# The third layer's block-diagonal products as quarters of the array, its messages and the projection by halves of the rows

## The chip, the cores and the metric

One Trainium2 chip; the program runs on one of its cores. The metric is the device time of one execution in microseconds (us). Of the kernel before there are three timed runs and one profiled execution.

## The reference

Four graph layers follow each other on x, which is 8 graphs x 2048 nodes x 64 features, with one shared 0/1 adjacency of 2048 x 2048. Each layer normalises, rectifies, computes and adds to x. The change is in the third layer and in what the third layer's last step prepares for the fourth. Cut to these:

```python
def _L2_gnn_ref(causal_vars, adj_matrix, intervention_value, W1, b1, W2, b2, intervention_idx):
    v = causal_vars.at[:, intervention_idx].set(intervention_value)
    for _ in range(3):
        effects = jnp.einsum('nm,bmd->bnd', adj_matrix, v)
        h = jnp.concatenate([v, effects], axis=-1)
        h = jax.nn.relu(jnp.einsum('bnk,dk->bnd', h, W1) + b1)
        v = jnp.einsum('bnk,dk->bnd', h, W2) + b2
    return v

def _L3_gnn_ref(x, adj, weight, a, bias):
    h = jnp.einsum('bni,io->bno', x, weight)
    e_src, e_dst = h @ a[:D, 0], h @ a[D:, 0]      # D = 64
    e = jax.nn.leaky_relu(e_src[:, :, None] + e_dst[:, None, :], negative_slope=0.2)
    ...                                            # times adj, softmax, times h

h = jnp.maximum(_layernorm(x, axis=-1), 0.0)
x = x + _L2_gnn_ref(h, adj, ...)
h = jnp.maximum(_layernorm(x, axis=-1), 0.0)
x = x + _L3_gnn_ref(h, adj, ...)
```

## The kernel before

**Layout.** Two graphs of 64 features make a pair, which fills the 128 partitions. There are NP = 4 pairs, called q. Features by node are kept as v(q), 128 partitions x 2048 nodes; the transposed form, by node, is u(t), 128 nodes x 512 columns (four pairs of 128), for each of NT = 16 tiles of nodes. A weight of 64 x 64 is placed twice on the diagonal of a 128 x 128 matrix (w1v, w1e, w2), with zeros elsewhere, so that one product serves both graphs of a pair.

**A step of the third layer.** The step's messages are v times the weight for neighbours. For each tile t, `messages` makes four products into one bank pn (128 nodes x 512) and empties it by one copy (step 0, taking turns between ScalarE and VectorE, L141 and L143) or by one addition on VectorE with the constant row later (steps 1 and 2, L1416). `split` then makes two parts of u, u_n_hi on ScalarE (L201) and u_n_lo on VectorE (L202), whose products with the adjacency run in one pass each. `adj_product` goes over NC = 4 chunks of 512 nodes. For a chunk it holds four banks pp0 to pp3, one for each pair. `first` begins them with the node's own product (w1v, or later in steps 1 and 2, which folds w2 and w1v); then come 16 tiles x 2 parts x 4 pairs of products with the adjacency (u_n in the text). `done` empties the four banks by Relu on ScalarE (L1444) into v, and at once makes the messages of the next step for the chunk's four tiles. In the third step `done` applies w2 instead, into banks named p2 (p in the trace), which VectorE adds to x (L1456), stores x and calls `Scores.chunk`.

**The projection.** `Scores.chunk` normalises the chunk for the fourth layer (center, to_rows, from_rows, the banks named bank) and multiplies each tile with wide, which holds weight3 twice on the diagonal and four columns for the scores: 132 columns, two pairs in one bank pw. Copies bring the features to rows(t) and the scores to scores; both go to f_rows in memory, from where the fourth layer gathers. `Scores.end` sums hn over all nodes and multiplies the sum with wide.

**The order.** A scheduler orders the instructions of each engine before the run, from the program's order and the buffers; the order on the chip is then fixed. Beside steps 0 and 1 runs a generator `neighbours`, one piece at every second tile of adjacency: it gathers 128 rows of the adjacency (L1486, POOL's queue, 1 MB each) into one of two buffers, and finds each row's neighbours by passes over 2048 columns on VectorE: L1490, L1494, then L1500 (eight highest) and L1503 (strike them out) in turns, and L1507 (copy). Fifteen tiles of rows pass through it.

**Buffers.** The banks pn and p2 have two buffers each. pw takes pn's, bank takes p2's.

All products on TensorE go through one helper, so they stand at L135 whatever they do; they are told apart by the names of their tiles. The listing shows the functions that the change touches.

Of the kernel before, what the change touches and what calls it, by code (L numbers as in the profile page):

```python
# [7 lines left out]
F = mybir.dt.float32  # L8
# [5 lines left out]
OP = mybir.AluOpType  # L14
# [5 lines left out]
P = 128  # L20
NB = 8
N = 2048
D = 64
NP = NB // 2
NT = N // P
R = P // NP
CW = 512
# [54 lines left out]
def columns(tile, s):  # L82

    return tile.rearrange("n (q s f) -> n q s f", q=NP, s=2)[:, :, s]
# [11 lines left out]
class Kernel:  # L96
# [36 lines left out]

    def mm(self, out, lhsT, rhs, start=True, stop=True):
        self.nc.tensor.matmul(out, lhsT, rhs, start=start, stop=stop)  # L135

    def copy(self, out, in_):

# [1232 lines left out]
    def layer2(self, slots):  # L1371
        nc, tc, a = self.nc, self.tc, self.a
        v = Halves(slots, "v", ("q0", "q1"), False)
        u = Halves(slots, "u", ("q2", "q3"), True)

        with (
            tc.tile_pool(reuse_waits="tile", name="k2", bufs=1) as k,
            tc.tile_pool(reuse_waits="tile", name="steps", bufs=2) as w,
            tc.tile_pool(reuse_waits="tile", name="steps_ps", bufs=1, space=PSUM) as ps,
            tc.tile_pool(reuse_waits="tile", name="steps_ps2", bufs=2, space=PSUM) as ps2,  # L1380
        ):
            w1v = self.block_diag(k, a["W1T"][:D], "w1v")
            w1e = self.block_diag(k, a["W1T"][D:], "w1e")
            w2 = self.block_diag(k, a["W2T"], "w2")

            w2n = k.tile([P, P], F, name="w2n")
            pw = ps2.tile([P, NP, P], F, name="pn")
            nc.tensor.transpose(pw[:, 0], w2, self.ident)
            nc.vector.tensor_copy(w2n, pw[:, 0])
            pw = ps2.tile([P, NP, P], F, name="pn")  # L1390
            self.mm(pw[:, 0], w2n, w1v)
            self.mm(pw[:, 1], w2n, w1e)
            self.mm(pw[:, 2], self.col("b2").to_broadcast([P, P]), w1e)
            self.mm(pw[:, 3, :1], w1v, self.col("b2"))
            later = k.tile([P, 3, P], F, name="later")
            nc.vector.tensor_copy(later, pw[:, :3])
            b1 = k.tile([P, 1], F, name="b1")
            nc.vector.tensor_add(b1, pw[:, 3, :1], self.col("b1"))
            own = [w1v, later[:, 0], later[:, 0]]
            seen = [w1e, later[:, 1], later[:, 1]]  # L1400
            bias = [self.col("b1"), b1, b1]
            full = [P, NP, P]
            for q in range(NP):
                nc.vector.tensor_copy(v(q)[:, 0:1], self.col("iv"))

            def messages(step, tiles):

                for t in tiles:
                    pn = ps2.tile(full, F, name="pn")
                    for q in range(NP):  # L1410
                        self.mm(pn[:, q], v(q)[:, t * P : (t + 1) * P], seen[step])
                    to = u(t).rearrange("n (q f) -> n q f", q=NP)
                    if step == 0:
                        self.copy(to, pn)
                    else:
                        nc.vector.tensor_add(to, pn, later[:, 2].unsqueeze(1).to_broadcast(full))  # L1416

            near = self.neighbours(k, slots) if self.short else iter(())
            last = Scores(self, slots, k, w, ps2) if self.short else None
            turn = [0]  # L1420

            def after(ch, m, at):
                turn[0] += 1
                if turn[0] % 2:
                    next(near, None)

            messages(0, range(NT))
            for step in range(3):
                if step == 2:
                    for _ in near:  # L1430
                        pass
                u_n = Split(slots, "u_n")
                for t in range(NT):
                    self.split(u_n, t, u(t))

                def first(ch, out, step=step):
                    s = slice(ch * CW, (ch + 1) * CW)
                    for q in range(NP):
                        self.mm(out[q], own[step], v(q)[:, s], stop=False)

                def done(ch, out, step=step):
                    s = slice(ch * CW, (ch + 1) * CW)
                    for q in range(NP):
                        nc.scalar.activation(v(q)[:, s], out[q], AF.Relu, bias=bias[step])  # L1444
                    if step < 2:
                        messages(step + 1, range(ch * TC, (ch + 1) * TC))
                        return
                    if last is not None:
                        x = last.x
                        nc.sync.dma_start(x, self.xs[2][ch])  # L1450
                    else:
                        x = self.load_x(w, 2, ch, bufs=1)
                    for q in range(NP):
                        p2 = ps2.tile([P, CW], F, name="p2")
                        self.mm(p2, w2, v(q)[:, s])
                        nc.vector.scalar_tensor_tensor(  # L1456
                            x[:, q], p2, self.col("b2"), x[:, q], op0=OP.add, op1=OP.add
                        )
                    self.store_x(2, ch, x)
                    if last is not None:  # L1460
                        last.chunk(ch)

                self.adj_product(u_n, w, ps, done, first=first, after=after)
            if last is not None:
                last.end()
# [371 lines left out]
class Scores:  # L1837
# [3 lines left out]
    def __init__(self, kern, slots, k, w, ps):  # L1841
        self.kern, self.nc, self.w, self.ps = kern, kern.nc, w, ps
        nc, a = self.nc, kern.a
        self.x, self.xr, self.sq, self.hn, self.total, self.rows = kern.last_slots(slots)

        self.wide = k.tile([P, P + 4], F, name="wide")
        nc.gpsimd.memset(self.wide, 0.0)
        self.sums = k.tile([P, NP, NC], F, name="sums")
        for s in range(2):
            half = slice(s * D, (s + 1) * D)  # L1850
            nc.sync.dma_start(self.wide[half, half], a["weight3"])
        wt = k.tile([D, 2, D], F, name="wt")
        for s in range(2):
            nc.sync.dma_start(wt[:, s], a["weight3T"])
        aa = k.tile([D, 2], F, name="aa")
        nc.sync.dma_start(aa, a["a2"])
        pa = self.bank()
        kern.mm(pa[:, :2], wt.rearrange("o s i -> o (s i)"), aa)
        for s in range(2):
            half = slice(s * D, (s + 1) * D)  # L1860
            for i in range(2):
                c = P + 2 * i + s
                nc.vector.tensor_copy(self.wide[half, c : c + 1], pa[half, 1 - i : 2 - i])

    def bank(self):
# [2 lines left out]
    def chunk(self, ch):  # L1868
        nc, kern = self.nc, self.kern
# [8 lines left out]
        kern.norm(ch, self.x, self.xr, self.sq, std, self.bank, write)  # L1878
        for t in range(ch * TC, (ch + 1) * TC):
            i = t - ch * TC  # L1880
            scores = kern.scores[:, t].rearrange("n (i q s) -> n q i s", i=2, s=2)
            for g in range(2):
                pn = self.ps.tile([P, 2, 256], F, name="pw", tag="pn")
                for j in range(2):
                    kern.mm(
                        pn[:, j, : P + 4], self.hn[:, 2 * g + j, i * P : (i + 1) * P], self.wide
                    )
                to = self.rows(t)[:, 2 * g * P : 2 * (g + 1) * P]
                kern.copy(to.rearrange("n (j c) -> n j c", j=2), pn[:, :, :P])
                nc.vector.tensor_copy(  # L1890
                    scores[:, 2 * g : 2 * g + 2],
                    pn[:, :, P : P + 4].rearrange("n q (i s) -> n q i s", i=2),
                )
            to = kern.f_rows[t * P : (t + 1) * P]
            nc.sync.dma_start(to[:, : NB * D], self.rows(t))
            nc.sync.dma_start(to[:, NB * D :], kern.scores[:, t])

    def end(self):
        nc = self.nc
        sums = self.w.tile([P, NP], F, name="all_sums", bufs=1)  # L1900
        nc.vector.tensor_reduce(sums, self.sums, axis=AX.X, op=OP.add)
        pt = self.bank()
        for q in range(NP):
            self.kern.mm(
                pt[:, q * P : (q + 1) * P], sums[:, q : q + 1].to_broadcast([P, P]),
                self.wide[:, :P],
            )
        nc.vector.tensor_copy(self.total, pt)


class Near:
# [345 lines left out]
```

## Time and profile before

| what | value |
|---|---|
| three timed runs | 2223.14, 2223.89, 2229.41 us; median 2223.89 |
| profiled execution | 2223.47 us, span 2221.7 us, clock 0.905 |
| TensorE, products | 1967.9 us busy, 7530 |
| TensorE, weight loads | 1187.1 us busy |
| VectorE, ScalarE, POOL | 1115.2, 708.9, 727.9 us busy |
| own products (w1v, later) | 96 passes of 512 columns |
| p (w2) | 32 passes of 512 columns |
| messages pn (w1e, later) | 384 passes of 128 columns |
| projection pw | 128 passes of 132 columns |

The span runs from the first to the last instruction of the profiled execution; 1.8 us lie around it. Busy time is a mean over four layers with different limits, so a cost is read from its stage: the third layer lies between about 1385 and 1925 us. A pass is one TensorE instruction; an fp32 product takes two. The mean duration of a pass in a group is from its start to its result and overlaps the next one's; the rate is read from the starts. In the timeline a row is a run of equal instructions: its start, the time it was busy, and how many; in brackets the idle time before it and what ended it.

### The profile page before, as it was taken

The numbers are of one execution on the slowest core, as the hardware profiler recorded it, in microseconds if no ns is written. First come the engines' busy times: TensorE is split into PE (matmuls) and PEld (weight loads), VectorE is DVE, ScalarE is ACT, GpSimd is POOL, SyncE is SP. The second block draws the span as 40 slices with busy tenths as digits, with TensorE's granted clock in tenths as the row PEclk, the third lists the DMA queues.
The fourth block names the chain that finished last, engine by engine and source line by source line (L and its number), as shares of the span: only waits on it lengthen the run. The fifth ranks groups of instructions, "written<-read, shape, count | busy, mean of one in ns | idle before, by whom it ended". The sixth has DMA issues, their size and how long they took to land.

```text
span 2221.7 us, 21410 instructions
## 1 busy us (share of the span) xinstructions
PE 1967.9 (89%) x7530; PEld 1187.1 (53%) x7530; DVE 1115.2 (50%) x1980; ACT 708.9 (32%) x1347; POOL 727.9 (33%) x609
## 2 busy tenths in 40 slices
PE   5877899987879989999999998998999999679873
PEld 1454766652226766353353532876777666345432
DVE  7846767744762032524425244988302222349762
ACT  6401455543444342020110200433434333258300
POOL 0012066755320002726537175011000000277760
PEclk8856899996777989999999998999999999789996
DMA  8231133451122453040130402456333443375655
GB/s 318 71 101 27 52 94 112 126 159 67 38 76 86 131 130 118 0 139 13 54 99 0 114 1 82 149 191 218 103 123 123 144 151 124 131 199 164 180 158 201
DMA packets 107742, 253.76 MB, mean 114 GB/s; under 512 B 19600, under 2 KB 19744, under 8 KB 100320
## 3 DMA queue, kind: packets, MB, share of 16 engines
q1 hardware_dynamic: 90000, 185.22, 26.1%
q0 software_dynamic: 17616, 67.00, 10.1%
q8 instruction: 63, 1.03, 0.2%
q14 instruction: 63, 0.52, 0.1%
HBM read 218.37 MB, written 33.81 MB: 114 GB/s over the span
## 4 chain that ended last, share of the span: by engine, by line
PE 57%; DVE 8%; POOL 7%; DMA 6%; issue 5%; ACT 3%; SPq 1%; POOLq 0%; DVEq 0%; ACTq 0%
PE pp L135 25%; PE pk L135 16%; PE bank L135 4%; POOL ring L1959 3%; PE acc L135 3%; PE pn L135 2%; PE p L135 2%; POOL q L1794 1%; DVE q L1809 1%; DMA q<-in_adj_dram,order 1%; POOL dt L632 1%; DMA adj_t<-in_adjT_dram 1%; PE pd L135 1%; PE po L135 1%; DMA ring<-f_rows,near 1%
## 5 line engine op out<-in xcount | busy, mean ns | idle before, releaser
L294 ACT CAST adj<-adj_t 128x512 fp32r<-128x512 f32 x384 | 236.7, 619 | 718.3 <-PE pp L135 625.2
L1353 POOL TENSOR_TENSOR acc<-acc,y 128x512 f32<-128x512 f32 x224 | 277.4, 1271 | 444.9 <-DVE y L1348 444.9
L135 PE MATMUL pk<-q,w 128*128 128x512 f32 (+1 forms) x1024 | 358.2, 612 | 9.9 <-DVE w L1270 8.9
L135 PEld LDWEIGHTS pk<-q,w 128*128 128x128 f32 (+1 forms) x1024 | 136.6, 188 | 228.0 <-issue 179.1
L135 PE MATMUL acc<-q,ident 128*128 128x512 f32 x416 | 205.1, 620 | 30.0 <-DVE q L2049 19.1
L1348 DVE SCALAR_TENSOR_TENSOR y<-pk,bias,q 128x512 f32<-128x512 f32 x224 | 157.7, 746 | 139.9 <-PE pk L135 130.3
L135 PE MATMUL pp<-adj,u_n_hi 128*128 128x512 f32 x768 | 217.2, 402 | 0.0
L135 PE MATMUL pp<-adj,u_n_lo 128*128 128x512 f32 x768 | 214.2, 398 | 0.0
L135 PEld LDWEIGHTS pp<-adj,u_n_hi 128*128 128x128 f32 x768 | 143.4, 188 | 39.0 <-issue 5.9
L1959 POOL DMA_INDIRECT ring<-f_rows,near x121 | 141.4, 1169 | 69.2 <-issue 57.4
L135 PEld LDWEIGHTS pp<-adj,u_n_lo 128*128 128x128 f32 x768 | 144.6, 188 | 34.5
L135 PEld LDWEIGHTS acc<-q,ident 128*128 128x128 f32 x416 | 77.1, 196 | 106.3 <-issue 48.8
L2063 POOL IOTA q<- 128x2048 int32 x1 | 1.8, 1835 | 355.3 <-PE p L135 355.3
L1794 POOL TENSOR_TENSOR q<-q,beta 128x512 f32<-128x512 f32 x57 | 67.6, 1188 | 104.8 <-DVE beta L1770 81.6
L135 PE MATMUL pp<-adj,x_ind_hi 128*128 128x512 f32 x256 | 95.5, 489 | 2.1 <-DVE q L700 1.9
L1348 DVE SCALAR_TENSOR_TENSOR acc<-pk,bias,q 128x512 f32<-128x512 f32 x32 | 22.6, 746 | 143.6 <-PE pk L135 143.6
L135 PE MATMUL bank<-std,from_rows 32*128 32x512 f32 x128 | 47.7, 938 | 41.8 <-DVE std L242 33.8
L135 PE MATMUL pp<-adj,h_n_hi 128*128 128x512 f32 x256 | 77.7, 416 | 0.0
L135 PE MATMUL pp<-adj,h_n_lo 128*128 128x512 f32 x256 | 75.3, 407 | 0.0
L2030 DVE TENSOR_TENSOR q<-ring,e 128x1024 f32<-128x1024 f32 x58 | 69.9, 1217 | 9.9 <-PE acc L135 9.7
L135 PE MATMUL pp<-adj,ah_n_hi 128*128 128x512 f32 x256 | 73.1, 405 | 0.0
L1416 DVE TENSOR_TENSOR q<-pn,later 128x512 f32<-128x512 f32 x32 | 21.5, 687 | 101.6 <-PE pn L135 101.4
(382 smaller groups left out, 3216.7 us busy)
## 6 DMA issues: line engine op xcount, KB each, us to landing
adj_t<-in_adjT_dram SPq DMA_DIRECT2D x160, 512.0 KB, 3.8
rows<-in_adj_dram SPq DMA_DIRECT2D x16, 1024.0 KB, 5.6
adj_t<-in_adjT_dram SPq DMA_DIRECT2D x64, 256.0 KB, 3.0
q<-x SPq DMA_DIRECT2D x12, 1024.0 KB, 5.0
q<-in_embT_dram SPq DMA_DIRECT2D x8, 1024.0 KB, 12.2
x<-q SPq DMA_DIRECT2D x8, 1024.0 KB, 3.9
x_ch<-in_xT_dram SPq DMA_DIRECT2D x4, 1024.0 KB, 6.2
h_rows<-q SPq DMA_DIRECT2D x16, 256.0 KB, 2.9
```

Of the source, the lines that this page charges most:

```text
L135: self.nc.tensor.matmul(out, lhsT, rhs, start=start, stop=stop)
L294: nc.scalar.copy(moving, at[:, i])
L632: nc.gpsimd.tensor_sub(dt, th[0], th[1])
L1348: nc.vector.scalar_tensor_tensor(y, pks[b, half], bias[:, b : b + 1], emb[:, b], op0=OP.add, op1=OP.mult,)
L1353: nc.gpsimd.tensor_add(acc, acc, y)
L1416: nc.vector.tensor_add(to, pn, later[:, 2].unsqueeze(1).to_broadcast(full))
L1794: self.nc.gpsimd.tensor_tensor(x, x, by.unsqueeze(2).to_broadcast([P, NB, D]), op=OP.mult)
L1809: nc.vector.tensor_add(d, d, self.pas.pop(i - 1))
L1959: self.nc.gpsimd.indirect_dma_start(to, None, self.kern.f_rows[:], bass.IndirectOffsetOnAxis(ap=index, axis=0))
L2030: nc.vector.tensor_tensor(y.rearrange("n i (b f) -> n i b f", b=NB), block[:, i : i + 2, : NB * D].rearrange("n i (b f) -> n i b f", b=NB) ...
L2063: nc.gpsimd.iota(whole, pattern=[[1, N]], base=0, channel_multiplier=0)
```

## The change

Where a product's weight is block-diagonal, its two blocks of 64 x 64 are now multiplied alone. A new helper `crosswise` makes four products for two pairs 2g and 2g+1, one for each quarter of the array: block r (rows 64r to 64r+63) of pair 2g+i goes to columns 64i to 64i+63 of bank 2g+r. This changes places between pairs; a second crossing changes them back. `first` and the product with w2 use it. Messages are made for each half of the rows on its own (64 rows, 64 columns), into two banks of 256 columns, one for each half, and emptied by two instructions of 256 columns; tiles take the buffers of pn and p2 in turns. The projection is made by halves too: wide is 128 x 66 without zeros, each half has a bank of four pairs x 66 columns, and two copies of features and two of scores empty a tile; before, as many did, for two pairs at a time. `end` makes eight products of 64 rows into two banks in place of four into one.

```diff
+    def crosswise(self, out, w, src, g, **kw):
+        for r in range(2):
+            h = slice(r * D, (r + 1) * D)
+            for i in range(2):
+                self.mm(out[r][i * D : (i + 1) * D], w[h, h], src(2 * g + i)[h], **kw)
...
             def messages(step, tiles):
                 for t in tiles:
-                    pn = ps2.tile(full, F, name="pn")
+                    pn = [
+                        ps2.tile([P, 2, 2, D], F, name="pn", tag=("pn", "p2")[t % 2])
+                        for _ in range(2)
+                    ]
                     for q in range(NP):
-                        self.mm(pn[:, q], v(q)[:, t * P : (t + 1) * P], seen[step])
-                    to = u(t).rearrange("n (q f) -> n q f", q=NP)
-                    if step == 0:
-                        self.copy(to, pn)
-                    else:
-                        nc.vector.tensor_add(to, pn, later[:, 2].unsqueeze(1).to_broadcast(full))
+                        for r in range(2):
+                            h = slice(r * D, (r + 1) * D)
+                            self.mm(
+                                pn[r][:, q // 2, q % 2], v(q)[h, t * P : (t + 1) * P],
+                                seen[step][h, h],
+                            )
+                    to = u(t).rearrange("n (g r c) -> n r g c", g=2, r=2)
+                    for r in range(2):
+                        got = pn[r].rearrange("n g i f -> n g (i f)")
+                        if step == 0:
+                            self.copy(to[:, r], got)
+                        else:
+                            nc.vector.tensor_add(
+                                to[:, r], got, later[:, 2].unsqueeze(1).to_broadcast([P, 2, P])
+                            )
...
-                    for q in range(NP):
-                        self.mm(out[q], own[step], v(q)[:, s], stop=False)
+                    for g in range(2):
+                        self.crosswise(
+                            out[2 * g : 2 * g + 2], own[step], lambda q: v(q)[:, s], g, stop=False
+                        )
...
-                    for q in range(NP):
-                        p2 = ps2.tile([P, CW], F, name="p2")
-                        self.mm(p2, w2, v(q)[:, s])
-                        nc.vector.scalar_tensor_tensor(
-                            x[:, q], p2, self.col("b2"), x[:, q], op0=OP.add, op1=OP.add
-                        )
+                    for g in range(2):
+                        p2 = [ps2.tile([P, CW], F, name="p2") for _ in range(2)]
+                        self.crosswise(p2, w2, lambda q: v(q)[:, s], g)
+                        for r in range(2):
+                            q = 2 * g + r
+                            nc.vector.scalar_tensor_tensor(
+                                x[:, q], p2[r], self.col("b2"), x[:, q], op0=OP.add, op1=OP.add
+                            )
...
-        self.wide = k.tile([P, P + 4], F, name="wide")
-        nc.gpsimd.memset(self.wide, 0.0)
+        self.wide = k.tile([P, D + 2], F, name="wide")
...
-            for g in range(2):
-                pn = self.ps.tile([P, 2, 256], F, name="pw", tag="pn")
-                for j in range(2):
+            pn = [self.ps.tile([P, NP, D + 2], F, name="pw", tag="pn") for _ in range(2)]
+            for q in range(NP):
+                for s in range(2):
+                    half = slice(s * D, (s + 1) * D)
                     kern.mm(
-                        pn[:, j, : P + 4], self.hn[:, 2 * g + j, i * P : (i + 1) * P], self.wide
+                        pn[s][:, q], self.hn[half, q, i * P : (i + 1) * P], self.wide[half]
                     )
-                to = self.rows(t)[:, 2 * g * P : 2 * (g + 1) * P]
-                kern.copy(to.rearrange("n (j c) -> n j c", j=2), pn[:, :, :P])
-                nc.vector.tensor_copy(
-                    scores[:, 2 * g : 2 * g + 2],
-                    pn[:, :, P : P + 4].rearrange("n q (i s) -> n q i s", i=2),
-                )
+            to = self.rows(t).rearrange("n (q s f) -> n s q f", q=NP, s=2)
+            for s in range(2):
+                kern.copy(to[:, s], pn[s][:, :, :D])
+                nc.vector.tensor_copy(scores[:, s], pn[s][:, :, D:])
...
-        pt = self.bank()
+        both = [self.bank() for _ in range(2)]
         for q in range(NP):
-            self.kern.mm(
-                pt[:, q * P : (q + 1) * P], sums[:, q : q + 1].to_broadcast([P, P]),
-                self.wide[:, :P],
-            )
-        nc.vector.tensor_copy(self.total, pt)
+            for s in range(2):
+                half = slice(s * D, (s + 1) * D)
+                self.kern.mm(
+                    both[s][:, q * D : (q + 1) * D], sums[half, q : q + 1].to_broadcast([D, P]),
+                    self.wide[half, :D],
+                )
+        for s in range(2):
+            nc.vector.tensor_copy(
+                columns(self.total, s), both[s][:, : NP * D].rearrange("n (q f) -> n q f", q=NP)
+            )
```

## The prediction

> **What bounds the kernel now.** I read the page's busy shares first, then its chain that ended last, then the chain in order of time over the third layer (about 1385 to 1925 us), and then the timeline at one boundary between two chunks of 512 nodes.
>
> ```profile
> PE 1967.9 (89%) x7530; PEld 1187.1 (53%) x7530; DVE 1115.2 (50%) x1980; ACT 708.9 (32%) x1347; POOL 727.9 (33%) x609
> ...
> PE 57%; DVE 8%; POOL 7%; DMA 6%; issue 5%; ACT 3%; SPq 1%; POOLq 0%; DVEq 0%; ACTq 0%
> ```
>
> TensorE is busy for 89% of the span and carries 57% of the chain. But the stage decides, so the chain in order of time:
>
> ```profile
> 1466.35 7.26 DMA q<-in_adj_dram,order
> 1473.64 2.35 DVE q L1490
> 1476.08 2.25 DVE q L1494
> ...
> 1510.42 9.06 DMA q<-in_adj_dram,order
> 1519.50 2.36 DVE q L1490
> 1521.88 2.29 DVE q L1494
> 1524.83 3.76 PE pn L135 x16
> 1528.60 30.66 PE pp L135 x128
> ```
>
> Until 1524.83 the path does not run over TensorE: it is the list of neighbours (row gather, L1490, L1494, L1500, one after the other), queued on VectorE ahead of the additions that empty the message banks. From 1528.6 on it is TensorE alone, up to the start of the last tail at 1897. So the change is priced on VectorE in step 0 and on TensorE afterwards. The timeline of TensorE at a boundary:
>
> ```profile
> 1440.78 1.88 PE L135 MATMUL pp<-q,w1v 128*128 128x512 f32 x4
> 1442.50 1.95 PE L135 MATMUL pn<-later,q 128*128 128x128 f32 x16
> 1444.28 1.02 PE L135 MATMUL pp<-q,w1v 128*128 128x512 f32 x2
> ...
> 1757.37 1.06 PE L135 MATMUL bank<-q,to_rows 128*32 128x512 f32 x8
> 1758.37 0.96 PE L135 MATMUL pp<-adj,u_n_hi 128*128 128x512 f32 x3
> ```
>
> An fp32 product is two passes. From start to start, four passes of 512 columns take 1.72 us (0.43 each, 0.86 a product), and 16 message passes 1.78 us (0.112 each). The eight passes of to_rows, which use four column groups, take 1.00 us together and not 8 x 0.43: packing works. The price of it is in a block of the second layer that mixes full products with pairs on 64 rows, and in its weight loads:
>
> ```profile
> 1305.42 22.26 PE L135 MATMUL pk<-q,w 128*128 128x512 f32 x64
> 1327.62 1.08 PE L135 MATMUL po<-acc,fold 128*64 128x512 f32 x4
> ...
> 1309.05 0.30 PEld L135 LDWEIGHTS pk<-q,w 64*128 64x128 f32 x4 [0.76 <-issue]
> 1309.59 0.19 PEld L135 LDWEIGHTS pk<-q,w 64*128 64x128 f32 x2 [0.23 <-issue]
> ...
> 1310.97 0.30 PEld L135 LDWEIGHTS pk<-q,w 128*128 128x128 f32 x2 [0.76 <-issue]
> ```
>
> The block takes 22.20 us from start to start. 32 full passes (13.76) and 16 pairs (6.88) explain 20.64. The other 1.56 us fall on eight changes between 128 and 64 rows, **0.2 us a change**: at each one the weights cannot be loaded ahead (idle 0.76 before the load, 0.23 inside a mode).
>
> **What the Trainium skill says.** "TensorEngine Tiling (Array Packing)", Key Properties: "Changing tiling mode (not just tile) drains the TensorE". The trace agrees, with the 0.2 us above. The same page, Gotcha 1, says that different row tiles must not write one PSUM bank at once; hence one bank for each half in the new code, and the pk pairs above have banks of their own. "TensorE: Matmul & The Clock Gate", section LDWEIGHTS: the load's time goes with the columns of the weights and not with the rows. The trace agrees: of po and pk, 64 rows x 128 columns take 186 ns in the mean, 128 x 128 take 190, 128 x 64 take 142. So halving the rows of a message's weights saves no load. "PSUM Bottleneck" on the tiling page: packing doesn't speed up the emptying of banks; the rows of L1416 and L143 bear it out below.
>
> **The change part by part.** The instruction order of the changed program (no time is in it) shows how its scheduler laid the pieces out.
>
> *Own products and the second weight.* 48 + 16 full products become 256 quarters. Packed in fours they would need 32 rounds of 0.86 us in place of 64. The order breaks the fours: around a chunk one quarter stands alone between messages, then one and three, then the rest. Counting rounds in which all quarters are on different places of the array, I get 4 at the start, 3 for each of three chunks of step 0, 4 into step 1, 3 for each of four chunks to step 2, and 5 for each of three chunks in step 2: 44 in place of 48. The second weight has 8 in place of 16. Saved: 12 x 0.86 = 10.3 us of TensorE.
>
> *Messages and projection.* Twice the products, in pairs on two row halves. The row at 1309.05 prices them: four loads of 64x128, two on each half, take 0.30 us where one takes 0.19, so the two halves load at the same time and the next pair follows 0.11 us later. Moving 64 columns takes less (a pass of 512 takes 0.43, so 64 some 0.05), so the loads set the pace. 384 message passes at 0.112 become 384 pairs at 0.107, and 128 projection passes at about 0.115 the same: -2.9 us. Bound from the other side: did the two halves load in turn, 512 x 0.107 = +55 us; that row excludes it.
>
> *Changes of mode.* From the order: 7 at the start, 7 for each of three chunks, 7 into step 1, 5 for each of four, 6 for each of three in step 2, and 9 for each of three projections (which stand in five blocks between adjacency products): 100. In 63 of them one side is the full array: 0.2 each, 12.6 us. The other 37 are between 64x128 and 64x64, which no row shows: at least 0, at most 0.2; I take 0.1, 3.7 us. So TensorE's own sum is -10.3 - 2.9 + 16.3 = +3 us, and what of it counts depends on the stage.
>
> *Step 0 (VectorE's path).* (1) Each message tile is emptied by two copies of 256 columns, one on each engine, where tiles took turns before. VectorE: 16 x 0.422 - 8 x 0.688 = +1.3. (2) The copy into later stands ahead of the first L1490 now. Before, L1490 ran from 1388.7 to 1391.1 while that copy waited for its product: +2.4. (3) At two chunk boundaries 8 additions of 0.687 become 16 of about 0.42: +1.2. (4) At the third boundary only L1490, no more L1494, stands ahead of the additions: -2.3. Sum +2.6. The gathers (7.3 and 9.1 us above) can fall worse behind a later chain: the first L1500 now stands behind all splits, and two lists go in step. I take +4, bounds -1 and +9. Queued behind the waiting L1490 are the additions, behind them the third and fourth message tile, and behind these the whole next chunk.
>
> *Into and through step 1 (TensorE's path).* Into step 1: no round saved, changes +0.9, messages -0.2: +0.7. Each of four later chunks: one round -0.86, changes 2 x 0.2 + 3 x 0.1, messages -0.16, and about +0.5 where the third tile waits for the first one's two additions (0.84 us against 0.69), because the products that filled this gap stand later now: +0.2. Together +1.5.
>
> *Step 2, three chunks.* The two rounds saved ahead of the norm are lost again to waits: the second quarter needs the second Relu (0.57 us later than the first), and the next two p2 tiles need both of the pair emptied (two L1456 of 0.75). Behind it, own products take three rounds for two, +0.86, and four changes +0.8. I take +1.3 a chunk (bounds +0.3 with no wait, +1.6). Projections: nine changes +1.8, pairs -0.25, but the blocks of eight hide waits for emptied banks that the order before had: its pw stretches at 1766.6 and 1866.4 last 6.9 us against 5.3 at 1817.3. I take +0.6. Sum +5.7, bounds 0 and +9.
>
> *Tail (last chunk).* Relu wait and p2 +0.4; a projection tile holds both banks, so that four tiles don't overlap with their emptying, +0.4: +0.8. Removed and hidden: one clearing on POOL (a gather queue with 39 us of idle ahead of it), and SP's queue keeps its transfers; two exchange places.
>
> The sum is 4 + 1.5 + 5.7 + 0.8 = +12 us. The profiled execution took 2223.5 us (span 2221.7), 0.4 under the median of the three, so **2235 us**.
>
> **Rivals.** *A, packing pays* (0.16): changes cost no more than half of what the full array shows, since the pipe would have run empty at a wait anyway, and the neighbour chain comes out early as in (4). Then -13.2 + 100 x 0.07, and 2 us off step 0: -8, about 2215. For it: eight products in 1.00 us at to_rows, and TensorE's path from 1528 to 1897. It decides from a mean change under 0.13 us. *B, a wash* (0.22): changes inside 64 rows are free and the gathers land early: step 0 at -1, step 1 at 0, step 2 at +2.5, tail +0.8: 2226. *C, the clock* (0.20): the messages of step 0 begin at half the clock (granted 0.50 from 1385 to 1391, and again from 664 to 680, where short transposes on 64 rows wait for their copies). If these thin products don't raise it, 128 pairs at 0.213 and four rounds at 1.72 end some 8 us later, and the neighbour list with them: 2243. For it: those transposes. Against: before, the clock is back after 6 us. *D, no packing of quarters* (0.02): 256 x 0.86 against 64 x 0.86, far over 2300. Against it stands to_rows. My own case has 0.40.
>
> **How the numbers follow.** A difference of 0.3% (6.7 us) is about what a measurement of this kernel can tell from no change. Slower by more: my case mostly, C and D: 0.60. Within: B and the lower end of mine: 0.24. Faster: A, 0.16. My own case spans 2227 to 2244 by the bounds above; the range takes in B, most of A and C: 2214 to 2250.
>
> **What would show it.** Right: the timeline shows groups of four p or pp passes starting together, pn pairs about 0.11 us apart, a gap of weight loads at each change, boundaries in step 1 still near 7 us, chunk tails of step 2 longer than 11.5 us, and additions of 256 columns near 0.42 us. The additions at the third boundary start after 1526. Wrong: boundaries in step 1 under 6 us (rival A), no idle at a change between pn and pp (rival B), a third boundary that ends before 1529, or a span longer outside 1385 to 1930.

## The result and the profile after

The changed kernel takes 2281.37 us (median of four runs, 2277.95 to 2283.35), the kernel before 2223.51 on the same chip: a ratio of 1.0254, 95% interval 1.0235 to 1.0274. It is 58 us slower, where 12 were forecast and the range ended at 2250. The profiled execution took 2283.35 us (span 2281.2).

The head of the page and three of its rows for 40 equal slices (57.0 us each; digits are tenths):

```profile
span 2281.2 us, 22764 instructions
...
PE 2015.9 (88%) x8178; PEld 1212.6 (53%) x8178; DVE 1116.1 (49%) x2021; ACT 711.1 (31%) x1355; POOL 728.2 (32%) x608
...
PEclk8756999986768989999999996899999898779996
```

TensorE's busy time grew by 48 us while its share stayed, and the other engines' work hardly changed. So TensorE did its work more slowly or did more of it. PEclk is the mean granted clock of each slice. Its 25th digit (slice 1369 to 1426) is a 6, and the next an 8: the first part of the third layer. The windows by stage say it exactly (stretch, its length, busy time and count of each engine, granted clock, DMA share, GB/s):

```profile
1393.00:1439.00 46.00, 46.00 (x284) 39.37 (x284) 22.07 (x41) 17.42 (x36) 0.94 (x1) 0.50 0.19 68
...
1599.00:1749.00 150.00, 149.39 (x832) 114.57 (x832) 29.31 (x54) 57.06 (x96) 0.00 (x0) 1.00 0.39 120
...
1864.00:1876.00 12.00, 11.22 (x88) 7.18 (x87) 4.43 (x17) 2.65 (x7) 0.00 (x0) 1.00 0.34 112
...
1916.00:1933.00 17.00, 16.22 (x86) 10.96 (x85) 4.42 (x17) 2.51 (x6) 0.00 (x0) 0.66 0.25 80
```

The first row is step 0's messages: 46 us in which TensorE's records leave no gap, VectorE and ScalarE are not busy all the time, and **the granted clock is 0.50 throughout**. (Records of passes overlap, so the array behind them can still pause.) In all traces here the clock is 0.50 or 1.00 and keeps a value for a multiple of 3.41 us, the "window" of the expectations below. The second is step 1, at full clock. The last two are the same work, the end of a tail of step 2 with its projection, once at full clock and once at 0.66. The chain in order of time, in which forecast and kernel before had VectorE's list of neighbours until the third boundary:

```profile
1414.41 20.67 PE pn L135 x176
1435.08 35.16 PE pp L135 x135
...
1550.59 9.37 DMA q<-in_adj_dram,order
1559.97 0.03 issue
1559.99 2.35 DVE q L1515
1562.34 0.34 DVE q L1434
1562.73 4.00 PE pn L135 x32
```

Now the messages on TensorE lead into it, and 176 passes take 20.67 us. The list returns to the chain only after the first chunk. At the third boundary L1515 (the former L1490) stands ahead of the additions (L1434), as the forecast said. TensorE at a boundary of step 1:

```profile
1675.00 0.66 PE L135 MATMUL pn<-later,q 64*128 64x64 f32 x8
1675.59 1.07 PE L135 MATMUL pp<-q,later 64*64 64x512 f32 x2
1676.59 3.72 PE L135 MATMUL pn<-later,q 64*128 64x64 f32 x56
1680.24 1.94 PE L135 MATMUL pp<-q,later 64*64 64x512 f32 x14
1682.11 1.20 PE L135 MATMUL pp<-adj,u_n_hi 128*128 128x512 f32 x4
```

Fourteen passes of quarters take 1.87 us from start to start, two rounds of 0.86 and 0.15: quarters run four at a time.

Where the layer's time went, from its product of w1v with w2n to its last projection, cut at the ends of the adjacency products (us; the last column is a kernel of the experiments):

| stretch | before | forecast | changed | two parts undone |
|---|---|---|---|---|
| to the end of step 1's first chunk | 209.6 | +4.7 | +32.6 | +3.2 |
| its other three and step 2's first | 149.1 | +0.8 | +0.5 | +0.5 |
| three further chunks of step 2 | 150.5 | +5.7 | +20.4 | +7.3 |
| last tail | 27.2 | +0.8 | +4.1 | +0.3 |
| layer | 536.4 | +12 | +57.6 | +11.3 |

Outside the layer the changed kernel's profiled execution has +7.3 us ahead of it and -5.4 behind it. These stretches hold the same work in all kernels here, but for a few products of `end`, and other profiled executions differ there by as much (1386 to 1398 us ahead of the layer), so the layer is what is compared.

### The profile page after: what moved, and what is told of

It is laid out like the page before. It is cut to its first block, busy times and chain, and to the rows that moved or that the text cites. A ratio compares the mean times of both kernels' runs of the same rounds, so it can differ in the third digit from the quotient of the medians.

```text
span 2281.2 us, 22764 instructions
## 1 busy us (share of the span) xinstructions
PE 2015.9 (88%) x8178; PEld 1212.6 (53%) x8178; DVE 1116.1 (49%) x2021; ACT 711.1 (31%) x1355; POOL 728.2 (32%) x608
## 4 chain that ended last, share of the span: by engine, by line
PE 58%; DVE 8%; POOL 6%; DMA 6%; issue 4%; ACT 3%; SPq 1%; POOLq 0%; DVEq 0%; ACTq 0%
PE pp L135 25%; PE pk L135 15%; PE bank L135 4%; PE pn L135 3%; PE acc L135 3%; POOL ring L1987 3%; PE p L135 2%; DMA q<-in_adj_dram,order 2%; POOL dt L640 1%; DMA adj_t<-in_adjT_dram 1%; POOL q L1819 1%; PE pw L135 1%; PE pd L135 1%; DVE q L1834 1%; PE pt L1235 1%
## 5 line engine op out<-in xcount | busy, mean ns | idle before, releaser
L302 ACT CAST adj<-adj_t 128x512 fp32r<-128x512 f32 x384 | 236.7, 619 | 745.3 <-PE pp L135 649.9
L1511 POOL DMA_INDIRECT q<-in_adj_dram,order x15 | 25.6, 1704 | 182.7 <-DVE top L1525 170.2
```

The lines of the kernel that those rows point to most:

```text
L302: nc.scalar.copy(moving, at[:, i])
L1511: nc.gpsimd.indirect_dma_start(row, None, self.a["adj"], bass.IndirectOffsetOnAxis(ap=order[:, 1, t : t + 1], axis=0),)
```

## The experiments

**What sets step 0.** The theory after the result: thin products leave the clock at one half. The rival: the copies by halves and their banks set the pace. Four kernels on one chip, where the kernel before took 2244 us (2233 to 2250); the layer's own length is compared. First, step 0's messages as whole products, with the copies as they are in the changed kernel:

```diff
+                    if step == 0:
+                        bank = ps2.tile([P, 2, 2, 2, D], F, name="pn", tag=("pn", "p2")[t % 2])
+                        for q in range(NP):
+                            self.mm(
+                                bank[:, :, q // 2, q % 2], v(q)[:, t * P : (t + 1) * P],
+                                seen[step],
+                            )
+                        ...
+                        for r in range(2):
+                            self.copy(to[:, r], bank[:, r].rearrange("n g i f -> n g (i f)"))
+                        continue
```

> The changed kernel, with the messages of step 0 alone made by the whole array again (128 rows x 128 columns, four products a tile); the two copies of 256 columns a tile, the quarters and the projection by halves stay. Theory of the clock: 64x64 products leave the clock at 0.50 for the whole 46 us of step 0's messages; with whole products it is back after two windows, the stretch from the first transposition of the layer to the end of the first chunk's adjacency falls from 78.2 to 53 to 57 us, and the total by about 23, to 2258. Rival theory, the copies by halves and the banks set the pace: the stretch stays near 78 us, the total near 2281.

Measured: 2270.11 us, a ratio of 1.0136 (1.0084 to 1.0188) to the kernel before on that chip, against 1.0254. The stretch of the expectation, 78.2 us changed, is 52.1, just under the 53 to 57 expected. From w1v with w2n on, the first chunk's stretch is 50.2 us against 75.5 changed and 49.9 before. Its windows, up to and after 1391:

```profile
1386.00:1391.00 5.00, 5.00 (x26) 5.00 (x25) 0.82 (x3) 1.06 (x3) 0.00 (x0) 0.51 0.96 387
1391.00:1413.00 22.00, 22.00 (x155) 18.32 (x155) 21.86 (x36) 16.41 (x37) 0.00 (x0) 1.00 0.20 64
```

With whole products the clock is back at 1391, and VectorE, with the same copies, is now busy for 21.86 of 22 us. The copies could go at that pace all along; the rival falls.

Next, what is it in a product that counts? All 128 rows, but 64 columns at a time:

```diff
+                            k = slice(None) if step == 0 else h
                             self.mm(
-                                pn[r][:, q // 2, q % 2], v(q)[h, t * P : (t + 1) * P],
-                                seen[step][h, h],
+                                pn[r][:, q // 2, q % 2], v(q)[k, t * P : (t + 1) * P],
+                                seen[step][k, h],
```

> The changed kernel, but each message product of step 0 takes all 128 rows and 64 columns (the zeros included), one after the other: 256 passes alone in place of 128 pairs. It asks what raises the clock. If rows or cells in use count: the clock is back after two windows, 256 passes at 0.107 are 27 us, the total about 2272. If the share of time in which columns stream counts (64 of some 128 that the weight load takes, half): the clock stays at 0.50, 256 passes at 0.213 are 55 us against 38, the total about 2298.

The same with 96 columns of the weight, of which the copies take the block's own 64 (run with the third set, where the kernel before took 2224.75):

```diff
+                            k = h
+                            if step == 0:
+                                k, h = slice(None), slice(r * 32, r * 32 + 96)
```

> The changed kernel, but each message product of step 0 takes all 128 rows and 96 columns, one after the other: the columns stream for 0.080 of the 0.107 us of a pass, three quarters, where 64 columns (one half) left the clock at 0.50 for 78 us and 128 columns brought it back in 10 us. If the limit lies under 3/4: half clock for 10 to 20 us, the first chunk's stretch near 60 us. If over it: half clock to the end of the messages, the stretch near 95 us as with 64 columns.

And half the rows in each product, still two at a time, but all 128 columns of the weight (banks and copies altered likewise):

```diff
-                                seen[step][h, h],
+                                seen[step][h, :] if step == 0 else seen[step][h, h],
```

> The changed kernel, but each message product of step 0 takes 64 rows and all 128 columns of the weight, the zeros included; the two halves of the rows still run as a pair, and the copies take the columns of their own block. If the share of streaming time counts for the clock: 128 columns fill the time of the weight load, the clock is back after two windows, 128 pairs at 0.112 to 0.133 are 14 to 17 us, and the total about 2258. If a product must have all rows to count: the clock stays at 0.50, the pairs take 0.22 to 0.27, and the total is 2277 to 2286.

The windows over step 0's messages, of the kernel with 128 rows x 64 columns:

```profile
1396.00:1464.00 68.00, 68.00 (x286) 60.47 (x287) 26.18 (x40) 18.05 (x37) 0.00 (x0) 0.50 0.10 35
```

of that with 128 rows x 96 columns:

```profile
1380.00:1400.00 20.00, 16.07 (x70) 12.72 (x71) 12.21 (x18) 3.30 (x8) 2.86 (x2) 0.57 0.69 238
1400.00:1410.00 10.00, 10.00 (x92) 10.00 (x91) 6.74 (x14) 6.09 (x13) 0.00 (x0) 1.00 0.16 54
1410.00:1420.00 10.00, 10.00 (x92) 10.00 (x91) 7.57 (x13) 4.78 (x11) 0.00 (x0) 1.00 0.00 0
```

and of that with 64 rows x 128 columns:

```profile
1381.00:1398.00 17.00, 14.35 (x74) 10.77 (x76) 10.40 (x18) 3.93 (x9) 1.91 (x2) 0.50 0.76 275
1398.00:1405.00 7.00, 4.78 (x66) 4.18 (x63) 7.00 (x11) 3.35 (x9) 0.00 (x0) 0.98 0.26 85
1405.00:1408.00 3.00, 3.00 (x28) 3.00 (x30) 3.00 (x5) 1.61 (x3) 0.00 (x0) 0.50 0.00 0
```

With 64 columns the clock never comes back before the messages end (first chunk 95.1 us), although every product uses all rows and TensorE leaves no gap in its records for 68 us. With 96 columns, and only the copies' reading altered with them, it is back at 1398 and stays for 65 us (first chunk 64.7). With half the rows and 128 columns it comes back too; it falls now and then for 3.4 us, where TensorE has waits for banks (L151) between the pairs. So the columns of a pass count, against the time that it takes. A pass of 512 columns takes 0.43 us at full clock, so 64 columns about 0.054 of the 0.107 us of a pass that its weight load sets (an estimate): one half is too little, three quarters (0.080) are enough. If it is the share, it has to be taken for each half of the rows: from 1417 to 1434 the two halves of the changed kernel's pairs start 0.06 us apart, so that one or the other streams for about 0.78 of the time (an estimate: 0.107 and 0.06 of 0.213), and the clock stays at 0.50.

Two rivals are left. All these passes take the time of one load, so a share of time and a number of columns per pass can't be told apart by them. And the products of half the rows ran mostly in pairs: a lone half with 128 columns was not tried.

Each of these kernels ran once. The totals of two of them, 2325 and 2295 us, lie 27 and 37 us over what was expected (2298 and 2258). The expectations were worked from 2281, on a chip where the kernel before took 2223.5, and step 2 had half clock in all three projections here; of the kernel with 128 columns the first chunk, too, took 62.5 us: at full clock its pairs follow each other at 0.112 us, but many passes stand alone, and TensorE waits for banks for 4.3 us in all. These misses don't touch the clock of step 0's messages, which did as one of the two theories said.

Last of this set, whole products ahead of the messages:

```diff
+            for i in range(10):
+                warm = ps2.tile([P, CW], F, name="warm", tag="pn")
+                self.mm(warm, w1v, v(i % NP)[:, 3 * CW :])
             messages(0, range(NT))
```

> The changed kernel with ten whole products of 512 columns (20 passes, results unused) ahead of the messages of step 0, to raise the clock first. They take about 12 us (half the clock for up to 7 us, then 0.43 a pass). If 64x64 pairs only fail to raise the clock but hold it: messages at 0.133 a pair, 17 us against 34, net 5 to 8 us faster than the changed kernel, about 2275. If they let it fall: the clock is at 0.50 again within one or two windows (3.4 to 7 us) of the first messages, and the total is 7 to 12 us longer, about 2291.

The ten products run from 1397.44 to 1407.3, then the messages. The windows:

```profile
1400.00:1413.00 13.00, 13.00 (x76) 8.10 (x74) 11.10 (x10) 2.67 (x6) 0.00 (x0) 1.00 0.14 49
1413.00:1437.00 24.00, 24.00 (x204) 21.82 (x206) 14.11 (x28) 11.90 (x25) 0.00 (x0) 0.51 0.01 1
```

The clock is full until 1413 and falls 6 us after the first message: thin products not only fail to raise the clock, they let it fall. The boundaries of step 1, where thin messages last 5.2 us between adjacency products of 30, keep it, which fits. The total was 2305.38 us, where about 2291 was expected (from the faster chip) if the clock falls. A loss of 7 to 12 us to the changed kernel does not show: the first chunk takes 72.1 us, 3.5 less. The ten products cost 9.8 us, but 56 message passes still ran at full clock and fewer of the others stood alone (26.2 us for all, in place of 34.0), the quarters among them took 4.2 us in place of 7.4, and the adjacency products behind had full clock from 1437 on, at once; in the changed kernel they had to wait 5 us for it.

**Which part loses what.** A second set (kernel before: 2225.59 us, 2218.20 to 2231.81). First only the halves, without quarters: messages of all steps and the projection as in the change, the pair's place kept (to = "n (q r f) -> n r q f"), own products and w2 as before.

> The kernel before with the messages of all steps and the projection by halves of the rows; own products and w2 stay whole products, no quarters. If the thin products by halves and the clock make the loss: nearly all of it is here, the third layer (from its product w1v with w2n to its last projection) about 585 to 592 us long against 536 before and 594 after, 50 us over before. If the quarters share it: under 570 us.

2280.66 us, a ratio of 1.0244 (1.0210 to 1.0278), the layer 598.9. The whole loss is here, and 7 us more than expected: a chunk of step 1 takes 38.08 in place of 37.20, where the order has four changes between halves and the full array at each boundary. Then only the quarters; each message product writes crosswise in one bank, as in the first diff, but for all steps and with one copy or addition, and the projection is as before.

> The quarters alone: own products and w2 crosswise as in the changed kernel; messages and projection by whole products as before, the crossing done by where the message products write in their bank. Theory: the clock stays as in the kernel before. A chunk of step 1 takes 36.9 us for 37.2 (three rounds of own products for four, less 0.3 for the changes of mode), a chunk tail of step 2 is 1.35 longer as in the changed kernel (w2 waits for its second pair), the layer 536 to 540 us: no difference from before that can be measured. Rival, quarters lose the clock too: half clock at boundaries of step 1, the layer over 550.

2240.78 us, 1.0062 (1.0040 to 1.0084); the layer 553.2, a chunk of step 1 38.23 in place of 37.20. Neither theory had this: in steps 0 and 1 the clock stays as it was, and the quarters alone still lose 1.03 us a chunk. (A chunk of step 2 takes 3.0 us more: 1.35 as expected, the rest from 17.1 us at half clock in that step, where the kernel before has 6.8.) TensorE's timeline at a boundary shows it:

```profile
1681.83 0.71 PE L135 MATMUL pn<-later,q 128*128 128x128 f32 x4
1682.47 1.07 PE L135 MATMUL pp<-q,later 64*64 64x512 f32 x2
1683.47 1.60 PE L135 MATMUL pn<-later,q 128*128 128x128 f32 x12
1685.00 1.08 PE L135 MATMUL pp<-q,later 64*64 64x512 f32 x4
1686.01 2.05 PE L135 MATMUL pn<-later,q 128*128 128x128 f32 x16
1687.99 1.93 PE L135 MATMUL pp<-q,later 64*64 64x512 f32 x10
```

One quarter product, then two, then five (two passes each) make four rounds, as many as four whole products; nothing is saved, and there are six changes of mode: 1.03 / 6 = **0.17 us a change**. In the changed kernel the order is one and seven, three rounds, so that its chunk takes 37.32.

Then the changed kernel with two parts undone: messages of step 0 as in the first diff, and the class Scores as before.

> The changed kernel with two parts undone: step 0's messages and the projection by whole products; messages by halves in steps 1 and 2 and all quarters stay. It is the changed kernel without the long half-clock stretches. If the forecast's sum was right but for the clock, the third layer takes about 546 us (before 536): +4 to the entry into step 1, +0.1 a chunk in step 1, +1.35 a chunk tail in step 2, +0.8 at the end. If the projection by halves cost nothing in the clock: 562 us, as with step 0's messages alone undone.

2232.63 us, 1.0035 (1.0015 to 1.0055), the layer 547.8: +11.3 us. It is the last column of the table above. In step 2 its chunks with as much half clock as before are 1.35 us longer (52.06 against 50.71), the forecast for the tail. The middle one, with 6.8 us at half clock where the kernel before has none, is 4.6 longer (53.67 against 49.09). So about 3.2 of the 11.3 are still clock.

Then quarters for the own products of steps 1 and 2 alone (first crosses if step is not 0; w2 needs no crossing then), all else whole.

> The kernel before with quarters for the own products of steps 1 and 2 only (two crossings, so that w2 needs none); all else by whole products. The version that should be best: a step 1 chunk 0.3 us shorter as in quarters alone, chunk tails of step 2 at most 0.4 longer or shorter (three rounds at two places), so 534 to 537 us for the layer, 0 to 2 us under the kernel before: same. Rival: changes of mode take the whole gain or more, 37.2 to 37.5 a chunk and 538 to 540.

2237.43 us, 1.0051 (1.0034 to 1.0068), the layer 546.7, a chunk of step 1 38.23: worse than its rival, and for the reason above. I had written down three rounds; the order had four (one quarter product, two, five).

**A version that gains.** If rounds and changes are what counts, the quarters of a chunk have to stand in one block. In a third set (kernel before: 2224.75 us in 25 runs), with quarters in steps 0 and 1 alone, and the messages of steps 1 and 2 by pairs over four banks:

```diff
+                banks = {
+                    t: ps2.tile([P, 2, 2, 2, D], F, name="pn", tag=("pn", "p2")[t % 2])
+                    for t in tiles
+                }
+                for q in range(NP):
+                    for t in tiles:
+                        ...
+                        self.mm(at, v(q)[:, t * P : (t + 1) * P], seen[step])
+                for t in tiles:
+                    ...
```

> The kernel before with quarters for the own products of steps 0 and 1 only (an even number of crossings), and in steps 1 and 2 the messages as whole products with the pair in the outer loop and four banks (those of pn and p2), so that all 16 stand first and the eight quarter products after them in one block: two rounds, two changes of mode. Projection and w2 as before. Theory (quarters pay only when their rounds are full and the changes few): a chunk of step 1 takes 1.72 less two rounds' worth of 0.3 for changes, 35.8 us against 37.2; the layer 529 to 532 us against 536; about 6 us under the kernel before (0.3%). Rival, the changes or the waits for the four Relus take it back: 37 or more a chunk, no gain.

2216.31 us, a ratio of **0.9958 (0.9942 to 0.9973)**; a chunk of step 1 35.86 us (35.8 expected), the layer 532.6 (529 to 532). Its timeline at a boundary:

```profile
1677.35 3.84 PE L135 MATMUL pn<-later,q 128*128 128x128 f32 x32
1681.12 1.95 PE L135 MATMUL pp<-q,later 64*64 64x512 f32 x16
1683.00 1.20 PE L135 MATMUL pp<-adj,u_n_hi 128*128 128x512 f32 x4
```

All eight quarter products take 1.88 us, two rounds and 0.16. The control has the same order of messages with whole own products:

> The control for the run with quarters in one block: the same order of messages (pair outermost, four banks), but own products whole, so that each chunk has 16 messages and then 4 own products, all of the whole array. If the gain there comes from the quarters, this one has chunks of step 1 near 37.2 us, as before; if it comes from the order of the messages, 36 us here as well.

2222.59 us, 0.9990 (0.9975 to 1.0005), chunks of step 1 at 37.2. So the gain is the quarters', once their rounds are full. Six chunks (three each of steps 0 and 1) are 1.35 shorter each than the control's; the layer's first chunk and the entry into step 1 give 3.7 of these 8.1 back. The first chunk begins with 3.8 us at half clock against 0.9 in the control, about 1.5 of the 2.1 us that it gives back; the rest is open. In both kernels the one long stall has moved from step 0's third boundary to the entry, where TensorE waits once on ScalarE's cast of the adjacency, for 10.9 us with the quarters (L302) and 7.8 in the control; what holds the cast up was not pursued.

## Why the prediction was wrong

**The step that failed is the price and the place of rival C, the clock.** It was named, but only as a rival: in the sum of 12 us it stands at nothing. It was held to step 0's messages, priced at 8 us and given 0.20. Measured: the first chunk's stretch grew by 25.6 us, and undoing that part alone gave 25.3 of it back; undoing the projection too brought the layer from +57.6 to +11.3. Behind that are three errors.

1. The counter-argument "before, the clock is back after 6 us" was taken from whole products. The halved ones were not the same case: by the estimate above 128 columns stream for the whole pass, 64 for half of it.
2. The evidence in the profile before was cut off at 680. Its windows go on (same columns as above):

```profile
672.00:680.00 8.00, 8.00 (x40) 4.67 (x42) 3.07 (x9) 4.26 (x11) 0.00 (x0) 0.50 0.28 87
680.00:690.00 10.00, 10.00 (x58) 5.90 (x59) 4.83 (x14) 4.54 (x13) 0.00 (x0) 0.50 0.00 0
690.00:696.00 6.00, 6.00 (x20) 4.48 (x20) 1.16 (x3) 1.36 (x3) 0.00 (x0) 0.53 0.27 90
```

   From 672 to 696 TensorE's records leave no gap; it mixes 64-column transposes with adjacency products, and stays at 0.50 until the adjacency products stand alone. The prediction put this down to waits for copies. A mixture is not the case of step 0, but a half clock without waits was there in full view.
3. The clock was thought of for step 0 only. The projection is thin too: where the clock falls just ahead of it, as it did in the kernel before for 3.4 us, it now stays down for 17.1 (why it falls there was not pursued), and two chunks of step 2 took 59.5 us where the one at full clock took 51.9: 7.6 us each. The same mixture kept full clock for the 8 us of that one, so it holds the clock that it finds. A sign of this was in the prediction, misread: the 6.9 us of two pw stretches against 5.3 of the third were put down to waits for emptied banks. The windows hold the same work, without a gap; the difference is the clock:

```profile
1766.60:1773.50 6.90, 6.90 (x41) 6.50 (x40) 2.79 (x14) 2.02 (x5) 0.00 (x0) 0.75 0.23 78
1817.30:1822.60 5.30, 5.30 (x41) 5.00 (x40) 2.79 (x14) 2.02 (x5) 0.00 (x0) 1.00 0.30 102
```

The working of C was short in its size as well. Its own figures, 128 pairs at 0.213 and four rounds at 1.72, make 34.2 us. The kernel before took 21.1 from its first message to the end of its messages (1389.63 to 1410.72), adjacency products among them, so at least 13 us more follow and not 8. Measured were 41.4 (1397.19 to 1438.61):

```profile
1397.19 7.20 PE L135 MATMUL pn<-w1e,q 64*128 64x64 f32 x40
1404.33 1.96 PE L135 MATMUL pp<-q,w1v 64*64 64x512 f32 x2
1406.22 6.29 PE L135 MATMUL pn<-w1e,q 64*128 64x64 f32 x32
```

In these two rows of messages most passes stand alone, 0.213 us each, the time of a pair, and the lone quarter takes a round of 1.9. The trace doesn't say which half a pass uses, so why they stood alone stays open.

**The sum without the clock came out near, in part by luck.** With the two thin parts undone the layer is 11.3 us over the kernel before; the forecast was 12. But that kernel has no projection by halves, for which 2.2 of the 12 stood (three times 0.6, and 0.4 in the tail), and 3.2 of its 11.3 are clock: 8.1 stand against 9.8. Point by point:

- *Step 0 and the entry into step 1*: +4.7 forecast; +4.4 with step 0's messages whole (first experiment), +3.2 with two parts undone.
- *Packing, rounds, groups.* Right: four quarters start 6 to 7 ns apart, rounds of 0.86, three rounds in a chunk of step 1.
- *Message pairs* 0.11 us apart: right at full clock (0.112). Not foreseen: in a row of 56 passes six stand alone and lose 0.3 us, so that the halves save nothing over whole products.
- *A change of mode*: 0.2 forecast against the full array, 0.17 found in the quarters alone. Between 64x128 and 64x64, 0.1 forecast: at 1680.24 the first quarter starts 0.20 us after the last message pass, where those are 0.11 apart, so about 0.09.
- *Step 1*: +0.2 a chunk forecast, 37.32 against 37.20 measured.
- *Tails of step 2*: +1.3 forecast, 12.84 against 11.49 measured (1787.26 to 1800.10). The projection at full clock took 8.1 us with 13 adjacency passes among it (1867.8 to 1875.9), before 5.3 with seven (1817.3 to 1822.6); six passes are 1.4, so it cost 1.4 more and not 0.6.
- *Additions* of 256 columns: 0.418 us, forecast 0.42; two of them take longer than the one of 512 columns before (0.687), so halves did not speed up the emptying of banks. At the third boundary only L1515 stands ahead of them, as forecast; the boundary waits 4.18 us for it.
- *Rivals.* A fell: boundaries in step 1 take 7.2 us, and changes cost 0.17. B fell: changes inside 64 rows are not free, and the kernel is 58 us slower. D fell: four quarters run at once. "Slower" at 0.60 was right in sign, but my own case had 12 of the 58 us; most of it came from C, which had 0.20.

## What to carry to other kernels

Before halving a product's columns, ask what share of its pass is streaming: here long runs of passes that stream for only half their time were held at half the clock however busy the engine looked. Price such a run at twice its time, and look in the trace before for any stretch at 0.50 in which TensorE's records leave no gap. Packing quarters of the array pays by full rounds and few changes: count both in the order of instructions, and give the block its place (more banks, the outer loop over what comes free first) before counting the gain. A sum of small terms can come within two microseconds and the forecast still be off by 46, when one state of the machine was left out of it.

## What the runs showed of the hardware

- "TensorE: Matmul & The Clock Gate" in the Trainium skill, Part 1, says that the clock is released after about 3.4 us of sustained activity. Here TensorE's records are without a gap for 46 us (64x64 pairs) and 68 us (128 rows x 64 columns), and the clock stays at 0.50. In passes that take the time of one load (0.107 us), 96 columns brought it back and 64 did not. Where between the two the limit lies was not tried.
- Full clock was lost 6 us after the start of such thin products, without a gap in the records.
- Thin projection products mixed with adjacency products kept the clock that they found: 0.50 for 17 us in two chunks, 1.00 for 8 us in another.
- Eight quarter products in one block take 1.88 us; a lone one, with its change of mode, 1.00. A change of mode costs about 0.17 us against the full array.
- A pass of 64 rows that stands alone takes as long as two side by side (0.213 us at half clock), so halves gain only where they run in pairs.
